# Final norm, gate and residual of a layer-1 FFN: per-head fused steps on VectorE in place of GpSimd additions, with a new written order

## The chip, the cores and the metric

The kernel runs on one core of one Trainium2 chip. A core has TensorE (PE, matrix products), VectorE (DVE), ScalarE (ACT), GpSimd (POOL) and SyncE (SP, which only issues DMAs here). Each engine works through its own instructions in their written order, and semaphores make one engine wait for another. The metric is the device time of one launch in microseconds (us), the median of several runs; less is better.

## What is computed

A small vision transformer: 32 images of 256x256 pixels become 256 tokens of 256 features each, two layers follow, everything is in float32. The change lies in the last part, the FFN of layer 1. Cut to what matters, with `x` the normed input of an image (256 x 256), 4 heads of 64 features and 4 experts:

```python
sx = einsum(x, hl_w) + hl_b                           # a 256x64 tile for each head
att = softmax(causal(q @ k * 8)); qkv = att @ v       # for 4 heads and 4 experts
mixed = sum over experts of qkv * softmax(gate(qkv))
fx = layernorm(mixed + resid, ln_g, ln_b)             # by head, 64 features
hx = relu(fx @ fc1.T + fc1_b) @ fc2.T + fc2_b         # by head
hx = layernorm(hx + fx, fnorm_g, fnorm_b)             # the final norm, by head
fg = softmax(hx.reshape(s, 256) @ fgate_w.T)          # a gate of 4 numbers for each token
h = h + hx * fg[..., None]                            # gate and residual
```

`fnorm_g` is all ones and `fnorm_b` all zeros in the inputs.

## The kernel before, in words

Tokens lie on the 128 partitions, two chunks (`NC`) for an image; four heads in two chunks make eight groups `g` of 64 columns, so a tile `[P, 8, 64]` holds an image. The residual stream `H[b]` of all images stays in SBUF. The first three stages (tokens, layer 0, attention of layer 1) are left as they are. They end at about 1243 us, and the layer-1 FFN fills the rest.

The FFN of an image is cut into 93 pieces, listed in `PIECES`. The number of a piece is its place in that list: 3 `heads`, 5 to 8 `experts`, 12 to 17 `scores` (TensorE), 18 to 23 `exponentials` (ScalarE, L1228), 24 to 29 `later_keys` (GpSimd selections for the causal mask, L1237), 31 to 38 `outputs` (TensorE), 39 to 46 their copies (ScalarE, L1257), 47 to 56 the softmax of the expert gate (VectorE, L1280 to L1314), 57 and 58 `mixed`, 59 to 61 `summed` (L1326, L1329, L1332), 62 to 66 norm and turn, 67 to 73 the two layers, 74 to 76 squares, their sum and the root for the final norm, 77 to 86 the final gate, 87 to 91 `last_norm`, 92 a move of features.

- `mixed` multiplies the experts' outputs by the gate: two experts on VectorE and two on GpSimd, both at L1318, 1024 columns each. `summed(0)` (L1326) adds the two halves.
- `head_gate` makes the final gate, a softmax over four numbers (L1434 to L1456, with an exponential on ScalarE at L1449). Its piece 9 (L1458) multiplies the inverse root by the gate.
- `last_norm` then has five pieces. VectorE scales by that product (L1463) and multiplies by the row `fn_g` (L1466). GpSimd makes `fn_b` times gate (L1469) and adds `H` (L1474) in its own tile `fadd`. VectorE adds `fadd` (L1477), and SP writes the image out (L1478).
- `turn_e` (L1360) turns the normed experts' result in blocks and sends it to DRAM, from where it comes back feature by feature. Its tile has the name `esq`, the same one buffer of the pool as that of `squares` (L1337).
- `check_ranges` (L1264, L1265) tests the ranges of sums once in eight images.

The order of the work is written out by hand: automatic scheduling is off, and the tuple `ROUND` gives pairs (back, piece). In round `r`, piece `k` is issued for image `b = r - back`, for all 93 pairs in turn. A round therefore touches six or seven images at different depths and finishes one image. This one sequence sets the order on every engine's queue, SP's included. When the heads of the last image are reached, `END` takes over, a sequence (images before the last, piece) that drains the pipeline.

Of the kernel before, what the change touches and what calls it, by code (L numbers as in the profile page):

```python
# [35 lines left out]
ALU = mybir.AluOpType  # L36
# [5 lines left out]
B, N, D = 32, 256, 256  # L42
# [38 lines left out]
def vit_tower(tc, a, out):  # L81
# [38 lines left out]
    def over(ap, shape, axis):  # L120
        return ap.unsqueeze(axis).to_broadcast(shape)
# [987 lines left out]
    with (  # L1109
# [10 lines left out]
        def whole(im, name, shape, pool=None, key=None):  # L1120

            key = key or name
            if key not in im.whole:
                im.whole[key] = (pool or p1).tile(shape, F32, name=name)
            return im.whole[key]
# [229 lines left out]
        def turn_e(b, im):  # L1355
            if b == B - 1:
                im.pt = feature_major(im.whole["er"].rearrange("p (c n) d -> p c (n d)", c=NC))
                return
            y = whole(im, "esq", G8, key="blocks").rearrange("p g d -> p (g d)")
            nc.vector.transpose(  # L1360
                y.rearrange("p (f s t) -> p s f t", f=4, t=32),
                im.whole["er"].rearrange("p (c k m) d -> p k c (m d)", c=2, k=2),
            )
            im.d = dram.tile([2, 4, 32, N], F32, name="er_turned", bufs=4)
            nc.sync.dma_start(im.d.rearrange("m i q x -> (i q) m x"), y.rearrange("p (m x) -> p m x", m=2))
# [65 lines left out]
        def head_gate(b, im, i):  # L1431
# [22 lines left out]
                nc.vector.reciprocal(im.m, im.m)  # L1454
            if i == 8:
                nc.vector.tensor_tensor(im.gate, im.gate, over(im.m, [P, NC, NH], 2), ALU.mult)  # L1456
            if i == 9:
                nc.vector.tensor_tensor(im.rs, im.rs, im.gate.rearrange("p c n -> p (c n)"), ALU.mult)  # L1458

        def last_norm(b, im, i):  # L1460
            if i == 0:
                f = whole(im, "fout", G8)
                nc.vector.tensor_tensor(f, im.whole["ey"][:, :, 0:HD], over(im.rs, G8, 2), ALU.mult)  # L1463
            if i == 1:
                f = im.whole["fout"]
                nc.vector.tensor_tensor(f, f, over(row_e("fn_g"), G8, 1), ALU.mult)  # L1466
            if i == 2:
                w = whole(im, "fadd", G8)
                nc.gpsimd.tensor_tensor(  # L1469
                    w, over(row_e("fn_b"), G8, 1), over(im.gate.rearrange("p c n -> p (c n)"), G8, 2), ALU.mult  # L1470
                )
            if i == 3:
                w = im.whole["fadd"]
                nc.gpsimd.tensor_tensor(w, w, H[b].rearrange("p c (n d) -> p (c n) d", d=HD), ALU.add)  # L1474
            if i == 4:
                f = im.whole["fout"]
                nc.vector.tensor_tensor(f, f, im.whole["fadd"], ALU.add)  # L1477
                nc.sync.dma_start(  # L1478
                    out[b].rearrange("(c p) d -> p c d", p=P),
                    f.rearrange("p (c n) d -> p c (n d)", n=NH),  # L1480
                )

        images = [Image() for _ in range(B)]
        PIECES = (
            (features_in,), (residual,), (moved_e,), (heads,), (heads_out,), (experts, 0), (experts_out, 0),
# [10 lines left out]
            (squares_sum, 0), (root, 0), (scaled,), (turn_e,), (turned_e,), (features_zero,), (first_layer,),  # L1496
            (first_layer_out,), (second_layer,), (second_layer_out, 0), (second_layer_out, 1), (squares, 1),
            (squares_sum, 1), (root, 1), (head_gate, 0), (head_gate, 1), (head_gate, 2), (head_gate, 3),
            (head_gate, 4), (head_gate, 5), (head_gate, 6), (head_gate, 7), (head_gate, 8), (head_gate, 9),
            (last_norm, 0), (last_norm, 1), (last_norm, 2), (last_norm, 3), (last_norm, 4),  # L1500
            (features_moved,),
        )
        ROUND = (
            (-11, 9), (-12, 6), (-10, 54), (-7, 85), (-10, 55), (-7, 86), (-10, 56), (-7, 87), (-10, 57),
            (-11, 30), (-13, 3), (-10, 58), (-11, 10), (-8, 69), (-11, 17), (-7, 89), (-8, 70), (-13, 4),
            (-13, 1), (-11, 25), (-11, 23), (-12, 12), (-11, 11), (-12, 16), (-7, 88), (-12, 22), (-10, 59),
            (-7, 90), (-11, 29), (-8, 68), (-13, 7), (-9, 2), (-12, 18), (-11, 36), (-10, 60), (-11, 27),
            (-10, 61), (-11, 33), (-11, 44), (-8, 71), (-11, 32), (-10, 62), (-13, 8), (-11, 31), (-11, 40),
            (-8, 72), (-11, 41), (-10, 63), (-8, 73), (-7, 91), (-8, 74), (-10, 64), (-12, 24), (-8, 75),
            (-11, 39), (-11, 34), (-8, 76), (-11, 38), (-11, 35), (-8, 77), (-11, 42), (-8, 78), (-11, 43),  # L1510
            (-11, 37), (-12, 14), (-11, 46), (-11, 45), (-10, 65), (-11, 47), (-8, 79), (-12, 28), (-12, 15),
            (-11, 48), (-8, 80), (-8, 81), (-11, 49), (-9, 67), (-12, 20), (-11, 50), (-12, 26), (-13, 5),
            (-8, 82), (-12, 13), (-11, 51), (-9, 92), (-11, 52), (-10, 66), (-8, 83), (-15, 0), (-11, 53),
            (-12, 21), (-8, 84), (-12, 19),
        )
        END = (
            (2, 10), (3, 58), (4, 2), (2, 25), (2, 27), (2, 11), (5, 69), (3, 59), (6, 88), (5, 70), (2, 17),
            (1, 16), (1, 9), (3, 60), (0, 4), (1, 10), (2, 31), (3, 61), (2, 23), (5, 68), (2, 36), (2, 39),
            (2, 33), (1, 22), (3, 62), (3, 63), (4, 67), (5, 71), (2, 35), (2, 29), (2, 38), (5, 72),
            (5, 73), (1, 11), (4, 92), (2, 34), (3, 64), (3, 65), (2, 37), (5, 74), (5, 75), (6, 89),  # L1520
            (2, 44), (2, 41), (1, 28), (2, 32), (2, 42), (6, 90), (1, 17), (2, 43), (3, 66), (5, 76), (0, 2),
            (6, 91), (2, 46), (2, 40), (5, 77), (5, 78), (5, 79), (2, 45), (2, 47), (2, 48), (5, 80),
            (1, 23), (2, 49), (1, 29), (0, 7), (5, 81), (2, 50), (1, 14), (2, 51), (2, 52), (2, 53), (5, 82),
            (4, 69), (2, 54), (2, 55), (0, 5), (0, 8), (1, 15), (5, 83), (4, 70), (1, 20), (2, 56), (1, 13),
            (5, 84), (2, 57), (2, 58), (0, 6), (0, 12), (1, 12), (1, 21), (1, 19), (0, 16), (0, 18), (1, 18),
            (3, 2), (4, 71), (4, 68), (2, 59), (1, 38), (1, 27), (2, 60), (4, 72), (2, 61), (1, 25), (1, 36),
            (1, 37), (4, 73), (1, 24), (0, 22), (1, 32), (2, 62), (1, 26), (1, 35), (0, 24), (3, 67),
            (5, 85), (2, 63), (5, 89), (1, 46), (4, 74), (1, 45), (2, 64), (5, 86), (1, 44), (5, 90),
            (1, 33), (5, 87), (4, 75), (4, 76), (3, 92), (5, 88), (2, 65), (2, 66), (1, 31), (1, 39),
            (1, 34), (1, 40), (1, 43), (1, 41), (1, 42), (1, 47), (1, 48), (1, 49), (0, 14), (4, 77),  # L1530
            (1, 50), (4, 78), (1, 51), (4, 79), (0, 20), (3, 69), (1, 52), (1, 53), (3, 70), (1, 54),
            (0, 15), (1, 55), (0, 13), (0, 9), (0, 26), (0, 17), (0, 21), (4, 80), (1, 56), (1, 57), (4, 81),
            (0, 10), (2, 2), (3, 68), (0, 11), (4, 82), (1, 58), (4, 83), (0, 23), (4, 84), (0, 31), (4, 85),
            (0, 19), (1, 59), (3, 71), (0, 25), (0, 27), (3, 72), (1, 60), (0, 30), (0, 33), (2, 67),
            (1, 61), (0, 32), (3, 73), (0, 34), (0, 28), (0, 39), (1, 62), (0, 35), (0, 43), (0, 29),
            (2, 68), (0, 36), (1, 63), (0, 40), (5, 91), (0, 42), (1, 64), (3, 74), (2, 92), (1, 65),
            (0, 44), (4, 89), (0, 37), (0, 38), (3, 75), (4, 86), (0, 41), (0, 46), (0, 45), (1, 66),
            (0, 47), (3, 76), (0, 48), (3, 77), (0, 49), (3, 78), (0, 50), (2, 69), (3, 79), (2, 70),
            (0, 51), (0, 52), (4, 87), (0, 53), (0, 54), (0, 55), (1, 2), (2, 71), (3, 80), (4, 90), (0, 56),
            (3, 81), (0, 57), (3, 82), (0, 58), (1, 67), (4, 88), (1, 69), (1, 92), (2, 72), (3, 83),  # L1540
            (0, 59), (3, 84), (0, 60), (3, 85), (0, 61), (4, 91), (0, 62), (2, 73), (1, 70), (0, 63),
            (2, 74), (0, 64), (1, 68), (2, 75), (2, 76), (0, 65), (2, 77), (3, 86), (2, 78), (2, 79),
            (3, 89), (3, 87), (2, 80), (0, 66), (2, 81), (1, 71), (2, 82), (3, 90), (0, 67), (3, 88),
            (2, 83), (1, 72), (2, 84), (3, 91), (2, 85), (1, 73), (0, 92), (1, 74), (1, 75), (1, 30),
            (1, 76), (1, 77), (2, 89), (2, 86), (0, 69), (1, 78), (2, 87), (1, 79), (1, 80), (2, 90),
            (1, 81), (2, 88), (0, 70), (1, 82), (1, 83), (0, 71), (1, 84), (2, 91), (1, 85), (0, 72),
            (1, 89), (0, 73), (1, 86), (0, 74), (0, 75), (1, 87), (0, 76), (0, 77), (0, 78), (0, 79),
            (1, 90), (0, 80), (0, 81), (1, 88), (0, 82), (0, 83), (0, 84), (1, 91), (0, 85), (0, 89),
            (0, 68), (0, 86), (0, 87), (0, 90), (0, 88), (0, 91),
        )  # L1550
        LATE = {1: B // 2 - 2, 2: B // 2 - 1}
        LAST = PIECES.index((heads,))

        def order_e():
# [422 lines left out]
```

## Time and profile before

| | before |
|---|---|
| median of 3 runs | 1882.4 us (1880.36 to 1883.76) |
| profiled execution | 1881.05 us |
| its span, first to last instruction | 1879.3 us |
| busy over the span | PE 97%, VectorE 72%, ScalarE 43%, GpSimd 44% |
| granted TensorE clock | 0.99 |
| FFN rounds, 1325.4 to 1772.6 us: busy of 447.2 us | PE 445.84, VectorE 408.17, ScalarE 351.09, GpSimd 295.20 |
| drain, 1772.6 to 1879.3 us: busy of 106.7 us | PE 74.29, VectorE 94.85, ScalarE 58.81, GpSimd 55.43 |

The profile page tells the busy time of each engine, the chain of work that ended last, and groups of instructions by source line. "DVE eo L1318" is the VectorE instruction that line 1318 issues, writing tile `eo`. `out<-in` names tiles, then shapes as partitions x elements, and a bracket at a row's end tells how long the engine idled before it and what ended that. The ends of matmuls are modelled, so a busy PE may stand still within its busy time.

### The profile page before, as it was taken

To read this page: it belongs to the slowest core of one execution; us is meant where nothing else is said; L and a number is where in the kernel's file an instruction comes from. 1 tells how busy PE (TensorE), PEld (TensorE's weight loads), DVE (VectorE), ACT (ScalarE), POOL (GpSimd) and SP (SyncE) were. 2 spreads that over 40 slices of the span, in tenths; PEclk is the share of its full clock that TensorE was granted. 3 is DMA by queue.
4 is the path that set the end of the run, shared out by engine and by line. 5 is a ranking of instruction groups with operands and counts; after the bars stand their busy time and mean duration, and the time that the engine had idled before them with its cause. 6 is when DMAs were issued, how large, how long until landed. Compare 5 with 4: busy or idle time off the path is not lost. (4 is left out here: it accounts for less than half of the span.)

```text
span 1879.3 us, 36625 instructions
## 1 busy us (share of the span) xinstructions
PE 1829.4 (97%) x14282; PEld 1286.5 (68%) x14282; DVE 1346.5 (72%) x3336; ACT 800.0 (43%) x1640; POOL 827.1 (44%) x792
## 2 busy tenths in 40 slices
PE   9999999999999999999999999999999999999993
PEld 7887567676767676766655555567877777787872
DVE  2335376878787674534578778746899989998998
ACT  0001222222222212121344554557878787877772
POOL 1224133434343334243353433424575757676653
PEclk9999999999999999999999999999999999999995
DMA  8540221212121134233222222122343333333332
GB/s 302 162 153 19 46 56 45 68 45 64 38 63 39 68 120 138 85 118 93 87 79 79 79 79 79 68 79 61 92 106 98 103 103 98 103 98 103 97 86 69
DMA packets 193171, 167.50 MB, mean 89 GB/s; under 512 B 70880, under 2 KB 166112, under 8 KB 192608
## 3 DMA queue, kind: packets, MB, share of 16 engines
q1 hardware_dynamic: 186272, 147.51, 27.3%
q0 software_dynamic: 6144, 16.79, 2.9%
q8 instruction: 115, 1.88, 0.4%
q10 hardware_dynamic: 576, 0.79, 0.1%
q14 instruction: 64, 0.52, 0.1%
HBM read 82.98 MB, written 57.41 MB: 75 GB/s over the span
## 5 line engine op out<-in xcount | busy, mean ns | idle before, releaser
L1237 POOL TENSOR_SCALAR_AFFINE_SELECT et<-et 128x1024 f32<-128x1024 f32 (+1 forms) x192 | 199.4, 1059 | 206.5 <-ACT et L1228 185.7
L118 PE MATMUL bank<-ev,et 128*64 128x72 f32 (+1 forms) x6144 | 204.2, 225 | 3.9 <-DVE ev L1203 2.3
L118 PEld LDWEIGHTS bank<-ev,et 128*64 128x64 f32 x6144 | 193.3, 137 | 17.7 <-POOL fadd L1474 7.6
L1228 ACT ACTIVATE et<-bank 128x512 f32<-128x512 f32 x384 | 199.6, 624 | 3.1 <-PE bank L118 1.7
L118 PE MATMUL bank<-g,sx 64*128 64x512 f32 (+1 forms) x512 | 194.4, 501 | 0.3 <-ACT g L1190 0.3
L118 PE MATMUL bank<-g,sw 64*128 64x512 f32 (+1 forms) x512 | 189.9, 501 | 0.9 <-DVE ev L1203 0.9
L118 PE MATMUL bank<-tokW,patch 128*128 128x256 f32 x768 | 166.6, 379 | 3.1 <-DMA patch<-in_patches_dram 3.1
L118 PEld LDWEIGHTS bank<-tokW,patch 128*128 128x128 f32 x768 | 145.9, 190 | 24.1 <-issue 3.9
L118 PE MATMUL bank<-bxT,w_wuv 128*128 128x512 f32 x300 | 131.4, 592 | 2.5 <-DMA bxT<-b_turned 2.5
L864 ACT ACTIVATE hT<-bank,cols 128x512 f32<-128x512 f32 x64 | 43.6, 687 | 187.3 <-PE bank L118 120.2
L118 PE MATMUL bank<-wvo,dm 128*128 128x512 f32 x256 | 114.3, 599 | 0.0
L118 PE MATMUL bank<-w_wo,gT 128*128 128x256 f32 x512 | 113.2, 379 | 0.0
L118 PE MATMUL bank<-attn,bv 128*128 128x256 f32 x512 | 113.1, 379 | 0.0
L118 PE MATMUL bank<-w_w,hT 128*128 128x256 f32 x512 | 112.3, 379 | 0.0
L118 PE MATMUL bank<-xsel,w_w 128*128 128x512 f32 x256 | 111.4, 592 | 0.0
L118 PEld LDWEIGHTS bank<-attn,bv 128*128 128x128 f32 x512 | 97.2, 190 | 19.6 <-issue 7.2
L118 PEld LDWEIGHTS bank<-g,sx 64*128 64x128 f32 x512 | 88.1, 186 | 31.4 <-issue 21.8
L126 DVE BATCH_NORM_STATS2 six<-h 128x6 f32<-128x256 f32 x256 | 105.6, 412 | 4.4
L118 PEld LDWEIGHTS bank<-w_w,hT 128*128 128x128 f32 x512 | 97.0, 190 | 15.6 <-issue 2.9
L118 PEld LDWEIGHTS bank<-w_wo,gT 128*128 128x128 f32 x512 | 97.2, 190 | 13.4 <-DVE gT L489 0.2
L151 POOL TENSOR_SCALAR rs_c<-st_c 128x4 f32<-128x4 f32 x16 | 3.0, 190 | 234.4 <-DVE st_c L127 234.4
L118 PE MATMUL bank<-w_wuv,bxT 128*128 128x512 f32 x240 | 105.4, 592 | 0.0
(289 smaller groups left out, 3814.6 us busy)
## 6 DMA issues: line engine op xcount, KB each, us to landing
patch<-in_patches_dram SPq DMA_DIRECT2D x31, 768.0 KB
exT<-normed SPq DMA_DIRECT2D x32, 256.0 KB
sw<-sx SPq DMA_DIRECT2D x64, 128.0 KB
out_dram<-fout SPq DMA_DIRECT2D x32, 256.0 KB
er_turned<-esq SPq DMA_DIRECT2D x31, 256.0 KB
fraw<-er_turned SPq DMA_DIRECT2D x62, 128.0 KB
both<-fxT SPq DMA_DIRECT2D x62, 128.0 KB
both<-hx SPq DMA_DIRECT2D x62, 128.0 KB
```

The costliest lines, as they stand in the source:

```text
L118: nc.tensor.matmul(o, lhsT, rhs, start=first, stop=last)
L126: nc.vector.bn_stats(six, x)
L151: nc.gpsimd.tensor_scalar(o, var, 1.0, 1e-5, ALU.mult, ALU.add)
L864: nc.scalar.activation(s.hT[:, m, :], p, AF.Gelu_apprx_tanh, bias=col("b1", m))
L1228: nc.scalar.activation(t2[:, i, :], p, AF.Exp)
L1237: nc.gpsimd.affine_select(out=own, in_=own, pattern=[[0, 2 * n_e], [1, P]], compare_op=ALU.is_ge, fill=0.0, base=0, channel_multiplier=-1,)
```

## The change

Four things are edited.

1. `head_gate(9)` goes; `last_norm(0)` uses the plain inverse root, so it no longer needs the gate.
2. `last_norm` runs on VectorE alone. Pieces 0 and 1 stay (scale, times `fn_g`); piece 2 adds the row `fn_b`; pieces 3 and 4 issue four fused instructions each, one for a head in a chunk: 64 columns of `f` times a gate value for each partition, plus the 64 columns of `H`. Piece 5 writes the image out. In the written order `fn_b` is added ahead of the multiplication by `fn_g`. `fadd` and both GpSimd instructions go.
3. `turn_e` gets a tile `eblk` of its own.
4. `ROUND` and `END` are new lists. `LATE` moves up in the text unchanged. In `PIECES`, number 86 is now `last_norm(4)`, the second half of the fused instructions, 90 the first half and 91 the write-out.

The core of the diff, the lists cut:

```diff
@@ -1356,7 +1356,7 @@
             if b == B - 1:
                 im.pt = feature_major(im.whole["er"].rearrange("p (c n) d -> p c (n d)", c=NC))
                 return
-            y = whole(im, "esq", G8, key="blocks").rearrange("p g d -> p (g d)")
+            y = whole(im, "eblk", G8).rearrange("p g d -> p (g d)")
             nc.vector.transpose(
                 y.rearrange("p (f s t) -> p s f t", f=4, t=32),
                 im.whole["er"].rearrange("p (c k m) d -> p k c (m d)", c=2, k=2),
@@ -1454,32 +1454,28 @@
                 nc.vector.reciprocal(im.m, im.m)
             if i == 8:
                 nc.vector.tensor_tensor(im.gate, im.gate, over(im.m, [P, NC, NH], 2), ALU.mult)
-            if i == 9:
-                nc.vector.tensor_tensor(im.rs, im.rs, im.gate.rearrange("p c n -> p (c n)"), ALU.mult)
 
         def last_norm(b, im, i):
+            f = whole(im, "fout", G8)
             if i == 0:
-                f = whole(im, "fout", G8)
                 nc.vector.tensor_tensor(f, im.whole["ey"][:, :, 0:HD], over(im.rs, G8, 2), ALU.mult)
             if i == 1:
-                f = im.whole["fout"]
                 nc.vector.tensor_tensor(f, f, over(row_e("fn_g"), G8, 1), ALU.mult)
             if i == 2:
-                w = whole(im, "fadd", G8)
-                nc.gpsimd.tensor_tensor(
-                    w, over(row_e("fn_b"), G8, 1), over(im.gate.rearrange("p c n -> p (c n)"), G8, 2), ALU.mult
-                )
-            if i == 3:
-                w = im.whole["fadd"]
-                nc.gpsimd.tensor_tensor(w, w, H[b].rearrange("p c (n d) -> p (c n) d", d=HD), ALU.add)
-            if i == 4:
-                f = im.whole["fout"]
-                nc.vector.tensor_tensor(f, f, im.whole["fadd"], ALU.add)
+                nc.vector.tensor_tensor(f, f, over(row_e("fn_b"), G8, 1), ALU.add)
+            if i in (3, 4):
+                for n in range(NH):
+                    g, d = (i - 3) * NH + n, slice(n * HD, (n + 1) * HD)
+                    nc.vector.scalar_tensor_tensor(
+                        f[:, g, :], f[:, g, :], im.gate[:, i - 3, n : n + 1], H[b][:, i - 3, d], ALU.mult, ALU.add
+                    )
+            if i == 5:
                 nc.sync.dma_start(
                     out[b].rearrange("(c p) d -> p c d", p=P),
                     f.rearrange("p (c n) d -> p c (n d)", n=NH),
                 )
 
+        LATE = {1: B // 2 - 2, 2: B // 2 - 1}
         images = [Image() for _ in range(B)]
         PIECES = (
             (features_in,), (residual,), (moved_e,), (heads,), (heads_out,), (experts, 0), (experts_out, 0),
@@ -1496,59 +1492,58 @@
             (squares_sum, 0), (root, 0), (scaled,), (turn_e,), (turned_e,), (features_zero,), (first_layer,),
             (first_layer_out,), (second_layer,), (second_layer_out, 0), (second_layer_out, 1), (squares, 1),
             (squares_sum, 1), (root, 1), (head_gate, 0), (head_gate, 1), (head_gate, 2), (head_gate, 3),
-            (head_gate, 4), (head_gate, 5), (head_gate, 6), (head_gate, 7), (head_gate, 8), (head_gate, 9),
-            (last_norm, 0), (last_norm, 1), (last_norm, 2), (last_norm, 3), (last_norm, 4),
+            (head_gate, 4), (head_gate, 5), (head_gate, 6), (head_gate, 7), (head_gate, 8), (last_norm, 4),
+            (last_norm, 0), (last_norm, 1), (last_norm, 2), (last_norm, 3), (last_norm, 5),
             (features_moved,),
         )
         ROUND = (
-            (-11, 9), (-12, 6), (-10, 54), (-7, 85), (-10, 55), (-7, 86), (-10, 56), (-7, 87), (-10, 57),
-            (-11, 30), (-13, 3), (-10, 58), (-11, 10), (-8, 69), (-11, 17), (-7, 89), (-8, 70), (-13, 4),
-            (-13, 1), (-11, 25), (-11, 23), (-12, 12), (-11, 11), (-12, 16), (-7, 88), (-12, 22), (-10, 59),
...
-            (-12, 21), (-8, 84), (-12, 19),
+            (-1, 77), (-1, 78), (-3, 62), (-1, 79), (-4, 33), (-4, 36), (-5, 27), (-4, 43), (-1, 80),
+            (-1, 81), (-4, 38), (-7, 0), (-1, 82), (-4, 32), (-4, 31), (-1, 87), (-4, 46), (-2, 2), (-1, 83),
+            (-4, 42), (-1, 89), (-4, 37), (-4, 41), (-1, 84), (-4, 44), (-6, 5), (-4, 40), (-1, 88),
+            (-4, 39), (-4, 45), (-5, 13), (-2, 67), (-1, 85), (-6, 6), (-1, 86), (-5, 28), (-5, 19),
+            (-1, 90), (-1, 91), (-5, 14), (-6, 30), (-4, 47), (-4, 48), (-5, 12), (-6, 7), (-2, 68),
+            (-5, 20), (-4, 49), (-6, 9), (-5, 25), (-4, 50), (-4, 51), (-4, 52), (-2, 69), (-5, 18),
+            (-3, 63), (-4, 53), (-5, 26), (-4, 54), (-2, 92), (-3, 64), (-7, 3), (-4, 55), (-4, 56),
+            (-6, 10), (-4, 57), (-2, 70), (-3, 65), (-6, 11), (-4, 58), (-3, 66), (-5, 24), (-6, 8),
+            (-5, 17), (-5, 23), (-6, 16), (-6, 15), (-4, 59), (-7, 4), (-7, 1), (-6, 22), (-5, 29), (-2, 71),
+            (-5, 34), (-6, 21), (-2, 72), (-2, 73), (-2, 74), (-4, 60), (-2, 75), (-2, 76), (-5, 35),
+            (-4, 61),
         )
         END = (
-            (2, 10), (3, 58), (4, 2), (2, 25), (2, 27), (2, 11), (5, 69), (3, 59), (6, 88), (5, 70), (2, 17),
...
+            (5, 70), (0, 2), (2, 17), (3, 55), (3, 56), (1, 8), (3, 57), (1, 16), (4, 65), (1, 10), (4, 66),
+            (0, 4), (1, 11), (3, 58), (2, 23), (2, 35), (2, 24), (3, 59), (2, 36), (1, 22), (3, 60), (5, 71),
...
+            (0, 86), (0, 91), (0, 1),
         )
-        LATE = {1: B // 2 - 2, 2: B // 2 - 1}

```

In the new round VectorE's order is: final gate of an image (77 to 86 and 90, with the three passes of `last_norm` among them), count of zeros, gate of the experts (47 to 56) of a younger image with a count of zeros and a sum of squares between, one half of the values, `mixed`, scale (65), other half of the values, turn (66), `summed(0)`, the second layer's two copies (72, 73), `summed(1)`, sum of squares (75), `summed(2)`.

## The prediction

> **What bounds the kernel now.** I read the page first. TensorE is busy nearly throughout, yet the chain that ended last runs through VectorE.
>
> ```profile
> PE 1829.4 (97%) x14282; PEld 1286.5 (68%) x14282; DVE 1346.5 (72%) x3336; ACT 800.0 (43%) x1640; POOL 827.1 (44%) x792
> ...
> DVE 22%; ACT 6%; PE 2%; issue 1%; ACTq 0%; DVEq 0%
> ```
>
> Next, the chain inside one stretch of the layer-1 FFN. The same instruction returns after 18.63 us, so that is one round (one image). The 4th mixing starts at 1325.4 us and the 28th at 1772.6: 24 rounds.
>
> ```profile
> 1604.98 2.86 DVE eo L1318
> ...
> 1609.87 2.21 DVE two L1326
> ...
> 1623.61 2.86 DVE eo L1318
> ```
>
> The windows view over those rounds (first row) and the drain (second): VectorE is 91% busy in the rounds, GpSimd 66%.
>
> ```profile
> core 0: us, PE busy (x) PEld busy (x) DVE busy (x) ACT busy (x) POOL busy (x), PEclk, DMA share, GB/s
> 1325.40:1772.60 447.20, 445.84 (x7157) 354.13 (x7156) 408.17 (x943) 351.09 (x866) 295.20 (x217) 1.00 0.39 100
> 1772.60:1879.30 106.70, 74.29 (x1210) 56.16 (x1209) 94.85 (x225) 58.81 (x146) 55.43 (x42) 0.82 0.30 81
> ```
>
> Much of that busy time is waiting. The timeline (start us, us) of two places, then durations by line (min/median/max ns):
>
> ```profile
> 1585.84 2.29 POOL L1318 TENSOR_TENSOR eo<-eo,gate 128x1024 f32<-128x1024 f32 x1 [0.43 <-DVE gate L1314]
> 1586.27 2.94 DVE L1318 TENSOR_TENSOR eo<-eo,gate 128x1024 f32<-128x1024 f32 x1
> ...
> 1590.67 1.70 POOL L1474 TENSOR_TENSOR fadd<-fadd,h 128x512 f32<-128x512 f32 x1
> ...
> 1591.17 2.29 DVE L1326 TENSOR_TENSOR two<-eo 128x1024 f32<-128x1024 f32 x1
> ```
> ```profile
> L1318 DVE TENSOR_TENSOR eo<-eo,gate x32: 1224/2940/2944, 1272.5 to 1841.3; 128x1024 f32<-128x1024 f32 x32
> L1326 DVE TENSOR_TENSOR two<-eo x32: 1207/2292/2295, 1280.8 to 1845.2; 128x1024 f32<-128x1024 f32 x32
> L1264 DVE SCALAR_TENSOR_TENSOR good<-ranges,good x4: 557/558/792, 1450.5 to 1864.5; 128x384 f32<-128x384 f32 x4
> L431 DVE SCALAR_TENSOR_TENSOR w_kept<-rank,cw x32: 146/153/1005, 264.6 to 700.9; 128x2 f32<-128x2 f32 x32
> ```
>
> L1318 on VectorE ends 1.08 us after GpSimd's half ends (1589.21 against 1588.13); L1326 ends 1.09 us after GpSimd's addition of H ends (1592.37). Undisturbed they take 1.2. So VectorE stands for 2.94-1.22 = 1.72 us behind GpSimd's mixing and for 2.29-1.21 = 1.08 us behind GpSimd's addition, every round. The waits view of 1344.0 to 1734.9 (21 rounds) gives what VectorE waits for ScalarE: (16.6+11.6)/21 = 1.34 us.
>
> ```profile
> DVE ranges L1341 <- ACT esq L1337: 16.6, 42, 0.4
> DVE lg L1434 <- ACT fv L1349: 11.6, 19, 0.6
> ```
>
> [...] here 512 columns cost GpSimd 1.04 and 1.26 us at least (L1469, L1474), VectorE 0.68.
>
> **VectorE's round, before.** Waits behind GpSimd: 1.72 + 1.08 + 0.29 (L1329, median 0.97 against 0.68) + 0.32 (L1332) + 0.27 (L1456, median 0.42 against 0.15) = 3.68. Own work: 18.63 - 1.34 - 3.68 = 13.6 us.
>
> **The change, part by part.**
> Removed from VectorE: the last addition L1477 (0.68, a step of 0.61 since the next starts 0.07 before its end) and gate times scale L1458 (0.11 step): -0.72. Removed from GpSimd: 1.04 + 1.26 us, and with them L1326's wait of 1.08.
> Added: the addition of fn_b, priced as its twin L1466 (1590.54 to 1591.17): +0.63. Eight fused instructions of 64 columns: from L431 (153 ns at 2 columns) and L1264 (558 at 384) the slope is 1.06 ns a column, so 219 ns[...]. Independent neighbours start some 0.065 us before the former's end (the pair L1287, 0.20 each, takes 0.32), so a step of 0.155: 8 x 0.155 + 0.07 = 1.3. Bounds: 0.09 a step if as cheap as L431, 0.24 if each waits for the former to end: 0.7 to 1.9. No kernel run shows this shape; I take 1.3.
> Own work after: 13.6 - 0.72 + 0.63 + 1.3 = 14.8.
> The fused steps wait for the gate of L1456, which hangs on ScalarE's exponential (0.24, L1449). L1463's 0.62 now stands between, so it is covered; uncovered it costs 0.24. Behind a late gate on VectorE stand the zero counts and L1280, and for those the expert gate and GpSimd's mixing.
> New order: the mixing of VectorE follows one copy-out of the values (L1203, 0.41) instead of L1463, while GpSimd's half starts 0.43 after the gate and takes 1.92 at least. Whichever gets in first, 1.1 and 1.8 us run one after the other before L1353 may: I keep 1.5. The selections (L1237, 0.63 or 1.08) remain and hit L1329, L1332 and L1353: 0.3 to 1.5, I take 1.0. ScalarE's answers now have cover: L1329 stands before the sum of squares, L1332 before the gate logits; I leave 0.2 of the 1.34. VectorE's round: 14.8 + 1.5 + 1.0 + 0.2 = 17.5.
> Own buffer of the turned result: it no longer shares the one buffer of the squares. Before, the wait there is data alone (ScalarE on L1332), so 0; if not, below 0.3. DMAs: 11 issues a round on SP as before. The output goes out just after the fused steps and its buffer is rewritten some 14 us later; the last output lands 4.8 us after issue (1874.5 to 1879.3), so it is hidden.
>
> **TensorE's floor.** Start to start, out of one round's timeline:
>
> ```profile
> 1592.59 1.68 PE L118 MATMUL bank<-ev,et 128*64 128x72 f32 x48
> ...
> 1594.10 1.12 PE L118 MATMUL bank<-W,both 128*64 128x68 f32 x32
> ...
> 1595.04 4.79 PE L118 MATMUL bank<-ev,et 128*64 128x72 f32 x144
> ```
>
> Outputs 1.51 + 4.56 = 6.07 (4.72 less a wait of 0.16), second layer 0.94; scores 8 pairs at 0.43 and 8 at 0.215, experts 8 at 0.215: 6.9; heads 8 x 0.215 = 1.7, first layer 0.86, values 0.95 (1603.31 to 1604.26). Sum 17.4. So about 1.2 us of TensorE's round is standing, hidden in modelled ends, and it is the next bound. ScalarE needs 351.09/24 = 14.6, GpSimd after the change 1.92 + 4.7: neither binds.
>
> **Sum.** With both at 17.4 to 17.5 and some friction I take a round of 17.65: 24 x 0.98 = -23.5 us. Range checks (2 x 0.56 us in 3 of the rounds) hid in ScalarE waits before, now partly not: +1.5. The fill up to 1325.4 has no final norm; its order is new: 0, between -3 and +3. Drain: the last gate is there at 1869.05 and VectorE ends at 1874.4, because GpSimd's 2.4 us and three full passes follow; now 1.3 follow, but 1.5 us of the flag's work comes into the open: -2.5. [...] Together -5, between -12 and +4. Total -27: profiled execution 1881.05 (span 1879.3 and 1.75 around it) to 1854; the median of the runs is 1.35 higher, so 1855.
>
> **Rivals.**
> (A) As above, 1843 to 1863: 60%.
> (B) [...] a selection queued ahead of GpSimd's mixing is released while VectorE makes the expert gate (L1303, two inputs) and blocks it for up to 0.95 us each round. For: L1456's 0.42 is such a hit. Against: then it waits for ScalarE most of the round (5.9 us). The round is then about 18.2: 24 x 0.43 = -10, drain -4, checks +1.5: 1870. 25%.
> (C) Slower: VectorE becomes the bound through the small instructions. From 0.30 us a step on (0.155 + 1.13/8) the gain is gone; at 0.4 the round is 17.5 + 8 x 0.245 = 19.5, 24 x 0.87 = +21 us, less some 3 in the drain: 1900. For: fixed cost is most of such an instruction[...]. [...] 8%.
> (D) No change: the round stays at 18.6 because an order that I can't price (TensorE waiting for exponentials or DMAs) takes the place: 1879 to 1886. 7%.
>
> **Numbers.** Faster by over 0.2% (about what a measurement of this kernel can tell from no change): A and B, 85%; same 7%; slower 8%. The range 1841 to 1873 takes in A, most of B, and a drain at its better end.
>
> **What would show it.** L1326 at about 1.2 us with few above; per-head instructions at 0.22 us starting 0.155 apart; mixing starts 17.5 to 17.9 apart; TensorE without standing time; VectorE's own waits for ScalarE under 0.3 a round. It is wrong if L1303 shows about 1.1 us (B), the fused steps lie 0.3 apart (C), or TensorE shows waits of over 1 us a round (D).

## The result, and the profile after

The changed kernel takes 1868.0 us (median of 4 runs, 1867.03 to 1871.56), the kernel before 1883.1 us beside it. The ratio is 0.9925, with a 95% interval from 0.9908 to 0.9943: 14 to 15 us faster, about half of the 27 forecast.

The page of the changed kernel, busy times and chain:

```profile
PE 1817.4 (97%) x14282; PEld 1277.9 (68%) x14282; DVE 1371.2 (73%) x3560; ACT 806.3 (43%) x1640; POOL 705.5 (38%) x728
...
PE 74%; DVE 17%; ACT 3%; DMA 2%; issue 2%; SPq 1%; DVEq 0%; ACTq 0%
```

Before, the chain, followed back over some 30% of the span, was mostly VectorE (22%, PE 2%). Now it reaches back over all of it and is mostly TensorE (74%), which VectorE (17%) joins here and there. VectorE is busy slightly longer than before, GpSimd 122 us less.

The windows view, cut at the same places as before (4th and 28th mixing, end):

```profile
core 0: us, PE busy (x) PEld busy (x) DVE busy (x) ACT busy (x) POOL busy (x), PEclk, DMA share, GB/s
1328.40:1765.00 436.60, 433.44 (x7153) 345.25 (x7152) 426.24 (x1112) 357.23 (x865) 193.15 (x169) 1.00 0.39 103
1765.00:1866.20 101.20, 71.30 (x1195) 53.10 (x1193) 92.53 (x265) 59.77 (x146) 33.63 (x25) 0.83 0.31 83
```

| stretch | before | after | difference | forecast |
|---|---|---|---|---|
| up to the 4th mixing | 1325.4 | 1328.4 | +3.0 | 0 (-3 to +3) |
| 24 rounds | 447.2 | 436.6 | -10.6 | -23.5, +1.5 for range checks |
| drain | 106.7 | 101.2 | -5.5 | -5 |
| span | 1879.3 | 1866.2 | -13.1 | -27 |

Of the +3.0, 1.6 us lie ahead of the FFN, in code that the change doesn't touch (attention ends at 1243.46 and 1245.08 us). The drain came as forecast here; in a second trace of the same kernel the first stretch is 1326.9 and the drain 103.4 us, so these two are known to some 2 us only, while the 24 rounds agree within 0.4 (436.2). The rounds gave less than half: 436.6/24 = 18.19 us a round instead of 17.65. Before, the rounds were nearly all 18.62 us. Now they run from 17.39 to 19.27 (17.4 seven times).

One of these rounds in the timeline (start us, us), beginning with the mixing:

```profile
1546.48 1.92 POOL L1318 TENSOR_TENSOR eo<-eo,gate 128x1024 f32<-128x1024 f32 x1 [0.35 <-DVE gate L1314]
1546.72 2.77 DVE L1318 TENSOR_TENSOR eo<-eo,gate 128x1024 f32<-128x1024 f32 x1
...
1549.40 1.11 DVE L1353 TENSOR_TENSOR er<-er,hv 128x512 f32<-128x512 f32 x1
...
1551.09 1.09 POOL L1237 TENSOR_SCALAR_AFFINE_SELECT et<-et 128x1024 f32<-128x1024 f32 x1 [1.11 <-ACT et L1228]
1551.47 1.78 DVE L1326 TENSOR_TENSOR two<-eo 128x1024 f32<-128x1024 f32 x1
...
1559.35 1.66 DVE L1469 SCALAR_TENSOR_TENSOR fout<-fout,fgate,h 128x64 f32<-128x64 f32 x8
```

VectorE's mixing again ends 1.09 us after GpSimd's half does (1549.49 against 1548.40). L1326, which used to stand behind GpSimd's addition of `H`, here stands behind a selection: it ends 1.07 us after the selection (1553.25 against 1552.18), where undisturbed it takes 1.2. In the 24 rounds L1326 is undisturbed in 12 (1.17 to 1.18 us) and takes 1.46 to 1.80 us in the other 12; before, it took 2.29 in 23 of them. Durations by line over all 32 images (min/median/max ns) and the waits view of 1345 to 1735 us:

```profile
L1326 DVE TENSOR_TENSOR two<-eo x32: 1174/1224/1795, 1279.8 to 1839.2; 128x1024 f32<-128x1024 f32 x32
L1312 DVE TENSOR_TENSOR gate<-gate,ranges x32: 150/169/722, 1275.4 to 1833.2; 128x32 f32<-128x32 f32 x32
```
```profile
DVE sm_m L1308 <- ACT gate L1305: 2.4, 5, 0.8
```

That one row is all that VectorE waits for ScalarE there, 0.1 us a round against 1.34 before.

### The profile page after: what moved, and what is told of

It reads as the page before. It is cut to its first block, busy times and chain, and to the rows that moved or that the text cites. A ratio compares the mean times of both kernels' runs of the same rounds, so it can differ in the third digit from the quotient of the medians.

```text
span 1866.2 us, 36505 instructions
## 1 busy us (share of the span) xinstructions
PE 1817.4 (97%) x14282; PEld 1277.9 (68%) x14282; DVE 1371.2 (73%) x3560; ACT 806.3 (43%) x1640; POOL 705.5 (38%) x728
## 4 chain that ended last, share of the span: by engine, by line
PE 74%; DVE 17%; ACT 3%; DMA 2%; issue 2%; SPq 1%; DVEq 0%; ACTq 0%
PE bank L118 74%; DVE fout L1469 2%; DVE eo L1318 1%; ACT et L1228 1%; DMA fraw<-er_turned 1%; DVE er L1353 1%; DVE two L1326 1%; DVE ranges L1341 1%; DVE junk L1172 1%; DVE ev L1203 1%; DVE er L1329 1%; DVE ey L1426 1%; DVE fout L1465 1%; DVE fout L1463 1%; DVE fout L1461 1%
## 5 line engine op out<-in xcount | busy, mean ns | idle before, releaser
L1237 POOL TENSOR_SCALAR_AFFINE_SELECT et<-et 128x512 f32<-128x512 f32 x192 | 197.6, 1038 | 309.4 <-ACT et L1228 308.6
L118 PE MATMUL bank<-ev,et 128*64 128x72 f32 (+1 forms) x6144 | 193.8, 224 | 1.9 <-DVE ev L1203 1.7
L118 PE MATMUL bank<-g,sw 64*128 64x256 f32 (+1 forms) x512 | 180.1, 490 | 1.2 <-ACT sx L1162 1.2
L118 PE MATMUL bank<-g,sx 64*128 64x512 f32 (+1 forms) x512 | 178.4, 490 | 0.0
L118 PEld LDWEIGHTS bank<-bxT,w_wuv 128*128 128x128 f32 x300 | 56.9, 190 | 67.9 <-issue 67.1
```

Source lines behind the costliest of these rows:

```text
L118: nc.tensor.matmul(o, lhsT, rhs, start=first, stop=last)
L1237: nc.gpsimd.affine_select(out=own, in_=own, pattern=[[0, 2 * n_e], [1, P]], compare_op=ALU.is_ge, fill=0.0, base=0, channel_multiplier=-1,)
```

## The experiments

"Round" below is the mean from the 4th to the 28th mixing, in each run's trace. The three parts are named: E, the new arithmetic of `last_norm`; O, the new lists; B, the own buffer.

| run | what it is | us, median | ratio to before (95%) | round |
|---|---|---|---|---|
| before | none | 1882 to 1883 | 1 | 18.63 |
| after_again | E, O, B | 1868.3 | 0.9926 (0.9912 to 0.9939) | 18.18 |
| own_buffer_only | B | 1883.8 | 1.0002 (0.9996 to 1.0009) | 18.65 |
| edit_old_order | E | 1915.6 | 1.0177 (1.0163 to 1.0191) | 19.72 |
| old_math_new_order | O, B | 1903.1 | 1.0103 (1.0087 to 1.0118) | 19.23 |
| shared_buffer | E, O | 1882.0 | 1.0001 (0.9992 to 1.0009) | 18.60 |
| full_passes | all, two full passes | 1868.8 | 0.9920 (0.9906 to 0.9934) | 18.16 |
| imm_scalar | all, constant scalar | 1870.7 | 0.9937 (0.9924 to 0.9951) | 18.23 |
| no_checks | all, no checks in rounds | 1867.1 | 0.9925 (0.9911 to 0.9938) | 18.15 |
| no_selections | all, no selections | 1860.8 | 0.9886 (0.9871 to 0.9901) | 17.91 |
| edit_old_nosel | E, no selections | 1865.4 | 0.9909 (0.9893 to 0.9926) | 17.87 |
| all_mix_dve | all, mixing on VectorE | 1861.7 | 0.9887 (0.9872 to 0.9903) | 17.94 |
| all_mix_full | the same, two full passes | 1861.0 | 0.9880 (0.9865 to 0.9895) | 17.89 |

The changed kernel ran once more with the others (`after_again`), and the kernels made out of the changed one are compared with that run.

> The changed kernel as it is, as the yardstick beside the others. Expected 1868 us (1866 to 1872), a mean round of 18.2 us between the 4th and the 28th mixing, rounds between 17.4 and 19.3 us, the eight fused instructions 0.196 us apart.

Measured: 1868.31 us (1868.11 to 1871.28), a span of 1866.6 and a round of 18.18 us.

### The new arithmetic in the old order

Here `ROUND` and `END` are those of before. Gate times scale is gone, the addition of `fn_b` stands directly behind the multiplication by `fn_g`, and the eight fused instructions at the place of the old last addition.

```diff
                 nc.vector.tensor_tensor(f, f, over(row_e("fn_g"), G8, 1), ALU.mult)
+                nc.vector.tensor_tensor(f, f, over(row_e("fn_b"), G8, 1), ALU.add)
...
-                nc.gpsimd.tensor_tensor(w, w, H[b].rearrange("p c (n d) -> p (c n) d", d=HD), ALU.add)
...
-                nc.vector.tensor_tensor(f, f, im.whole["fadd"], ALU.add)
+                for g in range(NC * NH):
+                    c, n = divmod(g, NH)
+                    nc.vector.scalar_tensor_tensor(
+                        f[:, g, :], f[:, g, :], im.gate[:, c, n : n + 1], H[b][:, c, n * HD : (n + 1) * HD], ALU.mult, ALU.add
+                    )
```

> The new arithmetic alone: the addition of fn_b and the eight fused instructions on VectorE, the GpSimd additions gone, but in the written order of before and with the shared buffer of the turned result. Theory (the edit alone costs VectorE more than it saves; the gain comes from the new order, which hides the waits for ScalarE): the round of 18.63 loses 1.08 (wait behind GpSimd's addition) and 0.72 (removed instructions) and gains 0.63 + 1.65, so 19.1 us; 24 x 0.47 = +11 us, 1890 to 1900 us, slower than before. Rival (taking the additions off GpSimd is what pays, the order only carries it): as fast as the changed kernel, 1864 to 1875 us, with L1326 at about 1.2 us in the trace.

Measured: 1915.6 us, 32 us slower than before, and more than the theory had. The round is 19.72 us instead of 19.1. The timeline shows why:

```profile
1567.45 1.11 POOL L1237 TENSOR_SCALAR_AFFINE_SELECT et<-et 128x1024 f32<-128x1024 f32 x1 [2.08 <-ACT et L1228]
1567.52 2.11 DVE L1326 TENSOR_TENSOR two<-eo 128x1024 f32<-128x1024 f32 x1
```

GpSimd's addition is gone, but a selection now starts 0.07 us ahead of L1326, and L1326 ends 1.07 us after it. It takes 2.11 us (median), hardly less than the 2.29 of before. Taking work off GpSimd didn't take the wait off VectorE: the next instruction in GpSimd's queue came into the same place. (The addition of `fn_b` had put L1326 back by 0.6 us; with `fn_b` elsewhere in the old list L1326 might have come first. That wasn't tried.) To see whether the selections were really the cause, they were taken out of this kernel.

```diff
-            own, n_e = im.own[k]
-            nc.gpsimd.affine_select(
...
-            )
+            pass
```

> The new arithmetic in the written order of before, with the shared buffer, and without GpSimd's selections; it leaves out the causal mask. With the selections this kernel had rounds of 19.77 us: L1326 still took 2.11 us, L1329 1.10 and L1332 1.00, although GpSimd's additions were gone. Theory (in the old order the selections move into the place of the additions and hold the same instructions up): L1326 1.2 us, L1329 and L1332 0.68 us, so 0.9 + 0.42 + 0.32 = 1.6 us less, a round of 17.9 to 18.3 us, 1865 to 1885 us. Rival (VectorE was late for another reason, ScalarE's answers in the old order): the round stays above 19 us, 1900 us or more.

Measured: 1865.4 us, 50 us less. The durations of the addition of the halves (L1326, here L1322) and the chain:

```profile
L1322 DVE TENSOR_TENSOR two<-eo x32: 1206/1218/1224, 1281.2 to 1824.9; 128x1024 f32<-128x1024 f32 x32
```
```profile
PE 89%; DVE 8%; ACT 1%; DMA 1%; issue 1%; SPq 0%; DVEq 0%; ACTq 0%
```

Every L1322 is now undisturbed, the round is 17.87 us, and the chain is TensorE's. So in the old order with the new arithmetic, the selections alone cost 50 us, and VectorE's own work, fused steps included, isn't what makes this kernel slow.

### The new order with the old arithmetic

The own buffer stays. Gate times scale, both GpSimd instructions, the scaling and the multiplication by `fn_g` stand together at piece 86; the last addition and the write-out are piece 91, moved seven pairs on in `ROUND`.

```diff
+                nc.vector.tensor_tensor(im.rs, im.rs, im.gate.rearrange("p c n -> p (c n)"), ALU.mult)
...
+                nc.gpsimd.tensor_tensor(w, w, H[b].rearrange("p c (n d) -> p (c n) d", d=HD), ALU.add)
...
-                nc.vector.tensor_tensor(f, f, over(row_e("fn_b"), G8, 1), ALU.add)
...
+                nc.vector.tensor_tensor(f, f, im.whole["fadd"], ALU.add)
...
-            (-1, 90), (-1, 91), (-5, 14), (-6, 30), (-4, 47), (-4, 48), (-5, 12), (-6, 7), (-2, 68),
+            (-1, 90), (-5, 14), (-6, 30), (-4, 47), (-4, 48), (-5, 12), (-6, 7), (-2, 68), (-1, 91),
```

> The new order alone: the arithmetic of before (gate times scale, two GpSimd additions, one full addition on VectorE) set into the places of the new lists, the write-out a few pieces later, own buffer of the turned result kept. Theory (the order is what pays): the waits for ScalarE (1.34 us a round) are gone and the round is 17.4 to 18.6 us, so 1858 to 1880 us, faster than before. Rival (removing the GpSimd additions is what pays): GpSimd's additions hold VectorE up as before and the round is 18.6 us or more, 1880 us or more.

Measured: 1903.1 us, 20 us slower than before; the rival's side. The timeline at the final norm:

```profile
1554.00 1.04 POOL L1462 TENSOR_TENSOR fadd<-rows_e,fgate 128x512 f32<-128x512 f32 x1 [4.21 <-DVE fgate L1456]
1554.09 1.50 DVE L1467 TENSOR_TENSOR fout<-ey,fv 128x512 f32<-128x512 f32 x1
1555.12 1.60 POOL L1465 TENSOR_TENSOR fadd<-fadd,h 128x512 f32<-128x512 f32 x1
1555.63 1.65 DVE L1468 TENSOR_TENSOR fout<-fout,rows_e 128x512 f32<-128x512 f32 x1
```

Both engines wait for the same gate and start together, so the two VectorE passes take 1.50 and 1.65 us where they take 0.68 in the changed kernel. My first theory, that the order pays by hiding ScalarE's answers, falls with this: before the sums of squares (L1341) VectorE now waits 0.07 us a round instead of 0.79, and the kernel is slower. What costs here is the additions: the two passes lose 0.82 and 0.95 us a round beside them. This holds for the places that the old arithmetic was given in the new lists; others weren't tried.

### The own buffer

```diff
-            y = whole(im, "eblk", G8).rearrange("p g d -> p (g d)")
+            y = whole(im, "esq", G8, key="blocks").rearrange("p g d -> p (g d)")
```

> The changed kernel with the turned result back in the one buffer that it shared with the squares. Theory (own buffer worth nothing, below 0.3 us a round): 1868 to 1875 us. Rival (without its own buffer the new order can't work, since turn and squares of two images now stand close together): a wait of more than 0.3 us in each round at the turn or at the squares, 1876 us or more.

Measured: 1882.0 us (13 runs), the time of before. The whole gain is gone. Waits and timeline of that kernel:

```profile
ACT esq L1337 <- DMA er_turned<-esq: 31.2, 21, 2.8
...
DVE ranges L1341 <- ACT esq L1337: 18.0, 19, 2.2
```
```profile
1556.20 0.69 DVE L1360 STREAM_TRANSPOSE esq<-er 128x512 f32<-128x512 f32 x1
...
1561.04 0.63 ACT L1337 ACTIVATE esq<-ey 128x512 f32<-128x512 f32 x1 [2.40 <-DMA er_turned<-esq]
1561.70 0.69 DVE L1341 TENSOR_REDUCE ranges<-esq 128x8 f32<-128x512 f32 x1 [1.76 <-ACT esq L1337]
```

The squares of the final norm want the buffer that the turned result is still being sent out of: 31.2/21 = 1.5 us of waiting by ScalarE a round, of which 18.0/21 = 0.86 reaches VectorE. The changed kernel has neither wait. In the trace of before, from the end of a turn to the start of the next squares it is 11.0 to 11.6 us; in the changed kernel it is 1.8 to 2.5. So it is the new order that needs the buffer. The other way round:

> The kernel before with nothing but an own buffer for the turned result. The shared buffer costs the new order 14 us. Theory (what it costs depends on the order: in the old list the squares of the next image come long after the turned result has been sent off, and what ScalarE waits for there is its data): no change, 1880 to 1885 us, a round of 18.63 us. Rival (the shared buffer held up the old order too, and the own buffer alone brings the gain of the whole change): 1866 to 1874 us.

Measured: 1883.8 us, ratio 1.0002, round 18.65. Alone, the buffer is worth nothing.

### What the fused steps cost

Two kernels make them cheaper. For the full passes and for the constant scalar (which leaves out the gate):

```diff
-                for n in range(NH):
...
+            if i == 4:
+                nc.vector.tensor_tensor(f, f, over(im.gate.rearrange("p c n -> p (c n)"), G8, 2), ALU.mult)
+            if i == 3:
+                nc.vector.tensor_tensor(f, f, H[b].rearrange("p c (n d) -> p (c n) d", d=HD), ALU.add)
```
```diff
-                        f[:, g, :], f[:, g, :], im.gate[:, i - 3, n : n + 1], H[b][:, i - 3, d], ALU.mult, ALU.add
+                        f[:, g, :], f[:, g, :], 1.0, H[b][:, i - 3, d], ALU.mult, ALU.add
```

> The changed kernel with the eight fused instructions replaced by two full-width passes on VectorE, times gate (read with a broadcast along 64 columns) and plus H. Theory (VectorE sets the round, each fused instruction costs 0.196 us): two passes of 0.61 + 0.61 instead of 1.65 us, 0.43 us less on VectorE in a round; where the round is above TensorE's floor of 17.4 us that is gained, so up to 24 x 0.43 = 10 us, and some 1 us in the drain: 1858 to 1864 us, faster than the changed kernel. Rival (TensorE or the selections set the round): no change, 1866 to 1870 us. Against both: a full pass with two SBUF inputs gives a selection a longer thing to be held behind or to hold, 1870 us or more.

> The changed kernel with the constant 1.0 in place of the gate's value for each partition in the eight fused instructions; it leaves out the multiplication by the gate in the output. It asks whether reading that value from a tile makes the instruction 0.28 us and its step 0.196 us, where 0.22 and 0.155 were forecast. If so: 0.22 us each, a step of 0.155, 0.33 us less in a round, and 0 to 8 us less in all (1860 to 1868 us). If not: 0.28 us and 0.196 us as before, 1868 us.

(In `full_passes`, `END` takes the two pieces of four late images in the reverse order, so that there `H` is multiplied too; the instructions are the same.)

Measured: 1868.8 and 1870.7 us, both the time of the changed kernel within the runs' spread. In `full_passes` the two passes take 1.42 us where the eight take 1.66; the addition of `H` has a median of 0.692 us and a maximum of 1.115. A selection can be held as well: in the changed kernel's rounds one of 512 columns that starts within VectorE's mixing takes 1.62 to 1.63 us, undisturbed 0.64. In `imm_scalar` the median instruction is 0.217 us instead of 0.279, and starts follow each other by 0.135 instead of 0.196: the eight take 1.17 us, 0.48 less of VectorE's round. None of either saving arrives at the end. Durations and waits of `imm_scalar`:

```profile
L1312 DVE TENSOR_TENSOR gate<-gate,ranges x32: 181/527/720, 1279.5 to 1838.4; 128x32 f32<-128x32 f32 x32
```
```profile
DVE sm_m L1308 <- ACT gate L1305: 7.6, 10, 1.1
```

L1312, the expert gate's product, has a median of 0.527 us instead of 0.169, and waits for ScalarE's exponential of the gate are up from 2.4 to 7.6 us. By round, over 24 rounds: L1312 +0.28, the wait before L1308 +0.22, L1303 +0.09, together 0.59, more than the 0.48 saved. By these rows, a VectorE that is early comes to the expert gate early, and there stands behind a selection or an exponential.

### The range checks

```diff
-            if i == 1 and b % 8 == 7 and b < B - 1:
+            if i == 1 and False:
```

> The changed kernel without the three range checks that fall into the rounds; it leaves out those three checks. Theory (they lie open in VectorE's round): three rounds shorter by 1.12 us, 3.4 us less, 1864 to 1866 us. Rival (a longer round is made up by the following ones, since TensorE has slack): 1867 to 1869 us.

Measured: 1867.1 us, 1.2 less than `after_again`; the 24 rounds take 435.6 us against 436.2 and 436.6 in the two traces of the changed kernel. Six instructions of 0.56 us disappear, 3.4 us in all, and less than half of that is gained. The interval doesn't separate it from the changed kernel.

### Without selections

The edit is the one shown above, made in the changed kernel.

> The changed kernel without GpSimd's selections; it leaves out the causal mask. Theory (selections queued on GpSimd hold VectorE up for 1.3 us a round, and uneven rounds come from where they fall): VectorE needs 16.9 us, TensorE's floor of 17.4 us sets every round, all rounds the same but those with range checks; 24 x 0.75 = 18 us less and a little in the drain, 1845 to 1853 us. Rival (what VectorE waits for is something else, and the selections only fill its gaps): rounds stay uneven with a mean above 17.9 us, 1860 us or more.

Measured: 1860.8 us. The first six rounds are even at 17.86 us, as the theory had it, and the others lie about it, between 17.0 and 18.9; but the level is 17.86 and not 17.4, so the gain is 7.5 us and not 18. VectorE did lose nearly what the theory said: the instructions of L1326, L1329, L1353 and L1312 are back at 1.18, 0.68, 0.68 and 0.14 us, together 1.2 us a round less. TensorE's timeline shows one period from outputs to outputs, then the chain:

```profile
1548.55 6.01 PE L118 MATMUL bank<-ev,et 128*64 128x72 f32 x192
1554.49 1.14 PE L118 MATMUL bank<-sx,A 64*128 64x256 f32 x8
...
1559.85 1.13 PE L118 MATMUL bank<-fxT,w_fc 128*128 128x512 f32 x2
1560.82 1.89 PE L118 MATMUL bank<-exT,w_hl_t 128*128 128x256 f32 x8
1562.63 0.48 PE L118 MATMUL bank<-g,sx 64*128 64x256 f32 x1
...
1566.41 0.77 PE L118 MATMUL bank<-ev,et 128*64 128x72 f32 x20
```
```profile
PE 92%; DVE 5%; DMA 1%; ACT 1%; issue 0%; SPq 0%; DVEq 0%; ACTq 0%
```

From 1548.55 to 1566.41 no row has a wait, and it is 17.86 us. By kind of product, mean of the 24 rounds and in brackets the forecast's figure: outputs 5.94 (6.07), second layer 1.00 (0.94), scores 5.36 (5.16), experts 1.84 (1.72), heads 1.82 (1.7), first layer 0.94 (0.86), values 0.98 (0.95); 17.88 against 17.4. The four kinds that the forecast had priced by a steady step (scores, experts, heads, first layer) are 0.08 to 0.2 us longer than that, together 0.52; the three that it had read as whole stretches differ by -0.13 to 0.06.

### A version faster than both

```diff
-            (nc.vector if k == 0 else nc.gpsimd).tensor_tensor(
+            nc.vector.tensor_tensor(
```

> The changed kernel with both halves of the mixing on VectorE. VectorE now spends 2.68 us on its half and 1.04 on the scaling behind it (L1353), of which 1.2 and 0.6 are own work. Theory (GpSimd's help at the mixing costs VectorE more than it saves): two halves of 1.2 and a scaling of 0.6 make 3.0 instead of 3.7 us; VectorE is then below 17.2 us a round and TensorE, at 17.9 us without the selections, sets it: 24 x 0.3 = 7 us less, 1859 to 1864 us. Rival (a selection that waited behind GpSimd's half now comes earlier and takes its place): 1.1 to 1.6 us in the mixing as before, so a round of 18.2 us or more, 1867 to 1880 us.

> As the run with both halves of the mixing on VectorE, and the eight fused instructions replaced by two full passes (times gate, plus H). Theory (VectorE is already below TensorE): no more than 2 us less than that run, 1857 to 1863 us. Rival (selections still make VectorE late in some rounds): the 0.3 us less on VectorE count in those, 2 to 7 us less than that run.

(`all_mix_full` always multiplies first.) Measured: 1861.7 and 1861.0 us, 6.6 and 7.3 less than the changed kernel and 21 to 22 less than before. The timeline of `all_mix_dve`, and its row of the mixing:

```profile
1544.50 1.47 DVE L1318 TENSOR_TENSOR eo<-eo,gate 128x1024 f32<-128x1024 f32 x1
1545.89 0.68 DVE L1353 TENSOR_TENSOR er<-er,hv 128x512 f32<-128x512 f32 x1
...
1546.89 1.21 DVE L1318 TENSOR_TENSOR eo<-eo,gate 128x1024 f32<-128x1024 f32 x1
```
```profile
L1318 DVE TENSOR_TENSOR eo<-eo,gate x64: 1199/1209/1633, 1278.5 to 1832.2; 128x1024 f32<-128x1024 f32 x64
```

Two halves on VectorE alone take about as long (2.63 us, mean of the rounds) as one half beside GpSimd (2.77), and the scaling behind is back at 0.68. Some of it returns: L1326's median rises to 1.90 us (1.22 in the changed kernel), behind a selection. The round is 17.94, and with the full passes 17.89, no faster than without selections: both are at TensorE's 17.9, and a cheaper VectorE brings no more.

## Why the prediction was right or wrong

**The sign and the range held; the likeliest time didn't.** 1868 lies outside case A (1843 to 1863) and beside case B's 1870. The mechanism was right in kind: with less waiting on VectorE the rounds come close to what TensorE needs. What TensorE needs was mis-sized.

**Right.** VectorE's reading of before. The cover for the gate and for ScalarE's answers: 0.1 us a round is left, 0.2 was taken. VectorE's wait at the mixing: forecast 1.5; the mixing takes 2.68 of the round; alone it would take 1.13 (1.21 less 0.08 of overlap), so 1.55. The selections: forecast 1.0, and L1326 (+0.25), L1329 (+0.31), L1353 (+0.44) and L1312 (+0.17) come to 1.17. In the 24 rounds of the trace, selections are all of GpSimd's work that lies beside any of the four, and in the kernel without selections all four are undisturbed. The write-out is hidden: VectorE waits for it once, 0.5 us. The drain gave 5.5 us in one trace and 3.4 in the other, for 5 forecast: 2.5 for the end after the last gate and, as the author's estimate, 2.5 for VectorE's waits behind GpSimd in the other late images. The two parts weren't told apart. The range checks, priced at 1.5, came out at 1.2, which the runs don't tell from nothing.

**Wrong: TensorE's floor.** "Sum 17.4" was 0.47 us too low. Four kernels, in two orders, with and without selections and with different work on VectorE, stop at 17.87 to 17.94, with TensorE at 80 to 92% of the chain. The steps of four kinds had been read inside stretches of one kind, and the passage from kind to kind was counted as standing time that could be won. From one image's first layer to the next, no round of TensorE between the 3rd and the 28th mixing is under 17.86 us in any trace of this case, and the changed kernel has six of just that length. The trace of before already shows one, with all kinds of product in it and no wait, between these two starts:

```profile
1309.37 1.02 PE L118 MATMUL bank<-fxT,w_fc 128*128 128x512 f32 x2
...
1327.22 1.02 PE L118 MATMUL bank<-fxT,w_fc 128*128 128x512 f32 x2
```

The round was set at 17.65, 0.15 above the larger of two figures (17.5), and with the range checks at 17.71. It came to 18.19, 0.32 above 17.87. By the forecast's own reckoning, of the 0.48 missing in a round 0.37 is the floor and 0.11 is friction that was taken too small: over 24 rounds 11.4 of the 13.9 us that the span falls short. The other 3.0 lie ahead of the rounds, and the drain gave 0.5 more than forecast.

**Wrong: the round as the larger of two sums.** With the measured terms put in, VectorE's sum after is not 17.5 but 18.0: the fused steps take 1.66 instead of 1.3 (inside the bounds of 0.7 to 1.9) and the selections 1.17 instead of 1.0. The overlap of neighbours was read well enough, 0.065 against 0.083 us; the instruction itself is 0.279 us and not 0.219. Yet making the fused steps 0.48 cheaper gained nothing, and so this mis-sized term by itself isn't what cost time. My reading is that the selections come when TensorE and ScalarE release them, so that VectorE's waits grow when it is early. It fits that 96 of the 144 selections of the rounds start on an idle GpSimd as ScalarE's exponential ends, and the rows of the constant scalar fit; but the release times weren't moved by themselves, so why the round stays 0.3 us above the floor is in part open. The savings that counted took away waits behind GpSimd: without selections 7.5 us, without GpSimd's half of the mixing 6.6.

**Wrong: "Own buffer of the turned result: 0".** In the new order it is worth 14 us, 1882.0 against 1868.3. In the old order the forecast's 0 is right (1.0002), and since the change has the own buffer, this miss didn't move the forecast time; it hid a part that the change can't do without. The step looked at what the squares wait for in the trace of before, their data, and took this over to an order in which they come nine us sooner after the turn. That the own buffer belongs to the new order could have been read from the new list: from piece 66 (turn) to the next 74 (squares) it is 17 pairs, where the old list has 57.

**Half right: GpSimd's additions.** Taking them off was to remove L1326's wait of 1.08. In the old order it doesn't: L1326 goes from 2.29 to 2.11. With the new list as well its median is 1.22 over all images, and half of the rounds still have a hit. The three parts aren't a sum: as placed here, the arithmetic alone costs 32 us, the order with its buffer 20, the buffer alone nothing, and together they gain 14 to 15.

**The rivals.** Case B gave the best number, with a round of 18.2, but not by its line: L1303 has a mean of 0.21 us and a maximum of 0.45 in the rounds. The hits of selections fall on L1312, L1326, L1329 and L1353, and B has nothing of TensorE's floor, which alone keeps the round at 17.87. That waits behind GpSimd move rather than go is half true; that the number fits so well is luck. Case C needed steps of 0.30; they are 0.196 (that they would come out below it was the author's estimate from L431, 0.153 us at 2 columns, and L1264, 0.558 at 384). Case D didn't come about.

In the changed kernel's rounds, what stretches beside a selection has two tensors as inputs: L1326 takes 1.46 to 1.80 us in the 12 rounds with a selection beside it and 1.17 to 1.18 in the other 12, and L1353 takes 1.11, where in the trace of before, with nothing of GpSimd beside it, it takes 0.68. The reduction from one input (L1341) has a selection beside it all 48 times, for 0.58 us of its time on average, and stays at 0.67 to 0.68 us.

## What to carry to other kernels

Taking an instruction off GpSimd need not take away the wait of VectorE behind it: here the next one in the queue came into its place (L1326 2.11 us instead of 2.29). Look at what is next, and when it is released. When an order is changed, go through every shared buffer with the distances of the new order, since a buffer that costs nothing at a distance of eleven microseconds cost 14 us here at a distance of two. And look for an engine's floor in a whole period without a wait, where the trace has one (here 17.86 us), and not in a sum of steady steps (17.4).

## What the runs showed of the hardware

- A fused VectorE instruction with two tensors of 64 columns takes 0.279 us with a scalar for each partition read from a tile, and 0.217 us with a constant; eight in a row start 0.196 and 0.135 us apart. The forecast, from shapes of 2 and 384 columns, was 0.219 and 0.155.
- On 1024 columns, a multiplication shared by VectorE and GpSimd holds VectorE for 2.77 us; VectorE alone makes both halves in two instructions with a median of 1.21 us each. With both on VectorE the whole kernel is 6.6 us faster.
